# Three orders of work in a masked linear layer with a gated FFN: a gate product behind three sums, the mask counted earlier, and first sums and weight sums moved

## The chip, the cores and the metric

The kernel runs on one core of a Trainium2 chip. The metric is the device time of one execution in microseconds (us); lower is better. Engines are named as the profile names them: PE is TensorE's matmul (PEld its weight load), DVE is VectorE, ACT is ScalarE, POOL is GpSimd and SP is SyncE, which issues almost all DMAs.

## The reference

All data is float32; 2048 rows of 512 features, an FFN with 1792 inner features.

```python
xn = _layernorm(x)
block_mask = mask.reshape(16, 32, 16, 32).astype(float32).sum(axis=(1, 3)) > 0
w_masked = weight * repeat(repeat(block_mask, 32, 0), 32, 1)
s = einsum('bsk,nk->bsn', xn, w_masked)

var = mean(square(xn), -1)
nx = xn * rsqrt(var + 1e-5) * ln_w
h = silu(nx @ gate_w.T) * (nx @ up_w.T)
g = silu(h @ down_w.T)
out = x + s * g
```

## The kernel before

**Tiling.** Every product is cut with two nested levels of a seven-product scheme: a 2x2 block product takes seven block products instead of eight, at the price of sums of blocks before and after. The outer level has seven products, numbered 1, 2, 6, 5, 7, 3, 4; each of them is again seven matmuls of a 128x128 weight block with a 128x512 block of data (m = 1 to 7). One outer product is an "instance" of seven matmuls (`instance`, L392 is its matmul). Gate and up projection and the masked linear layer are laid out alike: seven groups g = 0 to 6 hold the gate and up rows, group 7 is the masked linear layer. First the instances 1 and 2 of all groups run, then the instances 6, 5, 7, 3, 4 group by group. After that comes the down projection (`down_instance`, L640).

**Sums after the products.** An instance adds its matmuls into PSUM banks x, y and z. Between two matmuls of one bank a snapshot of the bank is taken to SBUF (`snap`), after its last one a total (`total`); both are one VectorE instruction of the helper `add` (L98), or a ScalarE copy where nothing is added. The next matmul into a bank whose snapshot is being taken waits for that snapshot. In a group, the quarter (1, 1) of the hidden block needs instance 5 plus instance 7: `summed` (L490) adds those two SBUF tiles, for quarters i = 0 and 1 on VectorE, for i = 2 and 3 on POOL.

**The gate.** When a gate tile and its up tile are there, ScalarE writes silu of the gate into a PSUM bank (`silu`, L458) and VectorE multiplies it with the up tile (`h_out`, L463) and stores the result to DRAM. The key (R, Hh, n) names quarter and column half.

**Order.** The order is written out by hand: `at(pos, fn, ...)` records a function with a position, all records are sorted by position at the end and issued in that order, with a stable order among equals; a manual schedule keeps it. One matmul is one unit of position, `T(us)` turns a time into a position. So a number in an `at` call decides only where an instruction stands in the queue of its engine. The engines run their queues in order and wait for each other by semaphores. DMAs go through SP's queue in the same way.

**Weights.** `load_a` fetches a gate and up tile for instances 1 and 2, `scale_a` (L311 on POOL, L313 on ScalarE) multiplies it with `ln_w`, `inner_a` forms four sums of weight blocks on POOL. A one-element memset on POOL (L739) holds back the loads of the group after the first, since they write the same tile. `load_block` and `outer_a` do the same for the other five instances; `inner_a(g, 2, ...)` then makes four POOL sums over five tiles at once (128x640).

**First data.** The first 1024 rows are normalised in place and transposed on TensorE; `inner_b` (from L779) forms sums of blocks of the transposed data, here partly with an operand in PSUM.

**Mask.** `load_mask` (L344) fetches four 128x512 tiles of the integer mask, `mask_rows` (L349) sums them over 32 columns on VectorE, `mask_blocks` sums over 32 rows by a matmul and compares with zero.

Of the kernel before, what the change touches and what calls it, by code (L numbers as in the profile page):

```python
# [31 lines left out]
def tile_masked_linear_gated_ffn(  # L32
# [36 lines left out]
    def at(pos, fn, *args):  # L69
        events.append((pos, len(events), fn, args))  # L70
# [18 lines left out]
    def slots(i, n):  # L89
        return mem[:, i : i + n, :]  # L90
# [3 lines left out]
    def bank(tag, name):  # L94
        return ps.tile([P, W], F32, tag=tag, name=name, bufs=PSB[tag])

    def add(eng, o, a, b, op=ALU.add):
        eng.tensor_tensor(o, a, b, op)  # L98

    dve, pool, act = nc.vector, nc.gpsimd, nc.scalar  # L100
# [193 lines left out]
    def w_slots(g):  # L294

        return (F["s"], F["s"] + 5) if g % 2 else (F["q"], F["a1"] + 4)
# [59 lines left out]
    def mask_a(v, R, K):  # L356
        v = v.rearrange("p (b j) -> p b j", j=BLK)
        k = keep[:, 2 * R + K, :].unsqueeze(2).to_broadcast([P, 16, BLK])
        nc.gpsimd.tensor_tensor(v, v, k, ALU.mult)

    def inner_a(g, part, k0=0, n=2):

        if part == 1:
            i, si, qs = F["a1"] + 2 * (g % 3), F["s"] + 2 * (g % 2), (1, 2)
        else:
            i, si, qs = *w_slots(g), BLOCKS
        a, s = slots(i + k0, n), slots(si + k0, n)
        a11, a21, a12, a22 = (a[:, :, k * P : (k + 1) * P] for k in range(4))
        s1, s2, s3, s4 = (s[:, :, k * P : (k + 1) * P] for k in range(4))
        for k in range(n):  # L370
            aop[g, qs[k0 + k]] = {1: a11[:, k], 2: a12[:, k], 3: s4[:, k], 4: a22[:, k],
                                  5: s1[:, k], 6: s2[:, k], 7: s3[:, k]}
        return [lambda: add(pool, s1, a21, a22), lambda: add(pool, s2, s1, a11, ALU.subtract),
                lambda: add(pool, s4, a12, s2, ALU.subtract), lambda: add(pool, s3, a11, a21, ALU.subtract)]
# [72 lines left out]
    def group(g, where):  # L447
        def tiles(i):
            return lambda k: mem[:, i + k, :]

        acc, v5, c1 = tiles(F["acc"] + 4 * (g % 2)), tiles(F["v5"] + 4 * (g % 2)), tiles(F["c1"] if g % 2 else F["vc"])
        vc = tiles(F["tmp"] + 2 if g % 2 else F["vc"])
        h11 = tiles(F["a1"])
        gate = {}

        def silu(key, t):
            gate[key] = bank("V", f"gate_{g}_{key[2]}")
            nc.scalar.activation(gate[key], t(), AF.Silu)  # L458

        hs, hpos = {}, {}  # L460

        def h_out(key, a, b, n):
            nc.vector.tensor_mul(a(), gate[key], b())  # L463
            hs[key] = a()
            q = {(0, 0): 1, (1, 0): 2, (1, 1): 3}.get(key[:2])
            if q:
                nc.sync.dma_start(h_dram[HD[q], g, n], a())

        def done(R, Hh, tiles):

            ready = {}

            def after(i, pos):
                r, n = divmod(i, 2)
                if g == G:
                    at(pos + 1, lambda: nc.sync.dma_start(s_dram[2 * R + r, 2 * Hh + n], tiles(i)))
                    return
                ready[i] = pos
                if n in ready and n + 2 in ready:
                    key = (R, Hh, n)  # L480
                    p = max(ready[n] + 1.2, ready[n + 2] - 0.5, SILU)
                    at(p, silu, key, lambda: tiles(n))
                    hpos[key] = max(p, ready[n + 2]) + 1.3
                    at(hpos[key], h_out, key, lambda: tiles(n), lambda: tiles(n + 2), n)
            return after

        def summed(dst, src, into, then=None, engines=(pool,) * 4):

            def after(i, pos):
                at(pos + 1.2, lambda: add(engines[i], into(i), dst(i), src(i)))  # L490
                if then:
                    then(i, pos + 3.2)
            return after

        nothing = lambda i, pos: None
        setup = {
            1: (None, acc, nothing),
            2: (acc, c1, done(0, 0, c1)),
            6: (acc, acc, nothing),
            5: (None, v5, summed(v5, acc, vc)),  # L500
            7: (acc, acc, summed(v5, acc, v5, done(1, 1, v5), (dve, dve, pool, pool) if g < G else (pool,) * 4)),
            3: (vc, vc, done(0, 1, vc)),
            4: (acc, acc, done(1, 0, acc)),
        }
        for q in setup:
            instance(where[g, q], g, q, *setup[q])

        def h_sum(q, n, tile_of, a, b):

            o = hs[q, n] = tile_of()  # L510
            add(pool, o, hs[a + (n,)], hs[b + (n,)], ALU.subtract)
            nc.sync.dma_start(h_dram[HD[q], g, n], o)

        sums, rest = slots(F["acc"] + 4 * (g % 2), 4), 7 * where[g, BLOCKS[0]]
        at(7 * where[g, 1] + 15, lambda: nc.sync.dma_start(acc_dram[g], sums))
        at(rest - (14 if g else 6), lambda: nc.sync.dma_start(sums, acc_dram[g]))
        if g < G:
            def again():
                nc.sync.dma_start(slots(F["a1"], 2), h_dram[HD[1], g].rearrange("n p w -> p n w"))
                hs.update({(0, 0, n): h11(n) for n in range(2)})  # L520
            at(rest + 24, again)
            pos = 0
            for n in (1, 0):
                for q, t, i, a, b in ((5, vc, n + 2, (0, 1), (0, 0)), (7, v5, n + 2, (1, 1), (0, 1)),
                                      (6, vc, n, (1, 1), (5,))):
                    pos = max(pos, hpos[0, 1, n], hpos[1, 1, n]) + 1.45
                    at(pos, h_sum, q, n, lambda t=t, i=i: t(i), a, b)
            for n in (1, 0):
                pos = max(pos, hpos[1, 0, n]) + 1.45
                at(pos, h_sum, 4, n, lambda n=n: acc(n + 2), (1, 0), (6,))  # L530
# [195 lines left out]
    T = lambda us: (us - 14.0) / 0.86  # L726
# [19 lines left out]
    def plan(pos, step, todo):  # L746
        for i, fn in enumerate(todo):
            at(pos + step * i, fn)
# [21 lines left out]
            at(T((8.9, 9.3, 9.8, 11.0)[c] + 0.05 * i), transpose, 0, c, (0, 1, 3, 2)[i], "XYYX"[c])  # L770
            at(T((14.35, 14.8, 15.25, 16.2)[c] + 0.05 * i), transpose, 1, c, (2, 3, 0, 1)[i], "XVVV"[c])
    at(T(6.0), scale_a, 0, 0, pool)
    at(T(10.0), scale_a, 0, 1, pool)
    for c in range(KC):
        at(T((9.75, 10.3, 10.85, 12.05)[c]), evacuate, 0, c, act)
        at((5.6, T(15.6), 6.0, 3.14)[c], evacuate, 1, c, act)
    for pos, q, m, eng in ((1.1, 1, 5, dve), (1.87, 1, 6, dve), (2.56, 1, 7, dve), (3.95, 2, 5, dve), (2.7, 1, 4, pool),
                           (4.6, 2, 6, dve), (7.2, 2, 7, dve), (5.0, 2, 4, pool)):
        at(pos, inner_b, q, m, eng)  # L779
    for q in (1, 2):  # L780
        for k in (0, 1):
# [39 lines left out]
    for g in range(G + 1):  # L821
        p, rest = 7 * where[g, 1], 7 * where[g, BLOCKS[0]]
        for K in range(2):
            if g > 2:
                at(p - 22, load_a, g, K)
            if g == G:
                at(p - (10.4, 7.3)[K], lambda K=K: mask_a(aq[G, 0, K], 0, K))
            elif g > 1:
                at(p - (10.4, 7.3)[K], scale_a, g, K)
        if g:  # L830
            plan(p - 7, 1, inner_a(g, 1))
        else:
            plan(T(9.9), 0, inner_a(0, 1, 0, 1))
            plan(T(11.9), 0, inner_a(0, 1, 1, 1))
        at(rest - 29, load_block, g)

        def block_sums(g=g):
            for k, fn in enumerate(outer_a(g)):
                todo[g, k] = fn
        at(rest - 20, block_sums)  # L840
        if g == G:
            for k, (R, K) in ((1, (1, 0)), (4, (1, 1)), (0, (0, 0)), (3, (0, 1))):
                at(rest - 20.5, lambda k=k, R=R, K=K: mask_a(wblk[G][k], R, K))
        for k, off in enumerate((-19.9, -19.3, -18.1, -17, -15.95, -15.94, -15.93, -15.3, -13.95)):
            at(rest + off, lambda g=g, k=k: todo[g, k]())
        plan(rest - 13, 2.5, inner_a(g, 2, 0, 5))
# [1 line left out]
        for off, fn in zip((8, 24.6, 26.05, 26.06, 26.07, 27.5, 30), outer_d(f)):  # L848
            at(7 * where[f, BLOCKS[0]] + off, fn)
    for i, (R, K) in enumerate(QUADS):  # L850
        at(50, load_mask, R, K)
        at(62 + 3.5 * i, mask_rows, R, K)
    at(79.5, mask_blocks)
    at(120, rms_store)
    for t in range(NTT):
# [10 lines left out]
    def D(o):  # L866
        return lambda k: free[25 * o + k] if 25 * o + k < 25 * len(DOWN) else free[25 * o + k - 1] + 1
# [6 lines left out]
    for o, q in enumerate(DOWN):  # L874
# [24 lines left out]
        for k in range(4):  # L899
            pos = END + (-6, -4.8, 2, 4)[k] if o == 0 else D(o - 1)(10) + 2.5 * k  # L900
# [84 lines left out]
```

## Time and profile before

| | |
|---|---|
| median of 3 runs | 510.52 us (510.2 to 510.72) |
| the profiled execution | 510.38 us, span of its instructions 508.6 us, granted clock 0.999 |
| matmuls of a 128x512 block (L392, L640) | 1126 instructions, two for each product, 0.43 us from start to start |
| VectorE, one 128x512 sum | 0.68 us, 0.60 from start to start |
| POOL, one 128x512 sum of two tiles | 1.27 us |
| POOL, one 128x640 sum of two tiles | 1.54 us |
| mask sums (L349) | 4 of 0.67 us, from 67.2 to 76.7 us |

A row of the timeline gives start, duration, engine, line and operation, `out<-in` by tile names, and `xN` where equal instructions follow each other without another kind between; in brackets the idle time before it and what ended it. Nearly all SBUF tiles lie in one large tile and have the name `mem`; `x`, `y`, `z`, `gate`, `a`, `held` and `pt` are PSUM banks. So `mem<-mem` reads SBUF alone, and `mem<-x,mem` reads a bank and an SBUF tile. Matmul durations overlap; the distance between starts is what counts. The page's line on POOL's and VectorE's busy shares says little about TensorE; its own stalls are seen in the starts of its matmuls.

### The profile page before, as it was taken

The page shows a single profiled execution, that of the slowest core. Times are in us where ns is not written, and L with a number is a line of the kernel's source. Part 1 is how long each engine was busy: PE and PEld are TensorE (multiplying, and loading weights), DVE is VectorE, ACT ScalarE, POOL GpSimd, SP SyncE. Part 2 cuts the span into 40 slices and gives each one's busy share as a digit, 9 for nine tenths or more (in the row PEclk, how much of TensorE's full clock was granted, in tenths as well). Part 3 has the DMA queues.
Part 4 walks back from the last instruction along what each step waited for, and adds up shares of the span by engine and source line. Part 5 has one row for each costly group of instructions (what it writes and reads, how often), then busy time and mean ns, then how long its engine had stood idle before and what let it go on. Part 6 is the DMA issues. An engine that isn't in the chain of part 4 may idle for free. (4 is left out here: it accounts for less than half of the span.)

```text
span 508.6 us, 4930 instructions
## 1 busy us (share of the span) xinstructions
PE 502.6 (99%) x1237; PEld 227.2 (45%) x1237; DVE 376.4 (74%) x583; ACT 188.4 (37%) x361; POOL 358.6 (71%) x300
## 2 busy tenths in 40 slices
PE   8999999999999999999999999999999999999996
PEld 7444434444444444444444444444444444444444
DVE  6978798776978969697796969969747644377636
ACT  5656776634535363352635334330100101001111
POOL 4628997473786959879596889976672764649960
PEclk9999999999999999999999999999999999999999
DMA  6758866269178495866939566599996798467362
GB/s 206 249 189 337 315 227 253 89 256 321 48 242 310 179 309 198 284 250 225 348 145 312 198 236 231 202 337 378 356 343 244 230 394 307 134 247 254 120 226 84
DMA packets 62221, 124.75 MB, mean 245 GB/s; under 512 B 5968, under 2 KB 13552, under 8 KB 60144
## 3 DMA queue, kind: packets, MB, share of 16 engines
q1 hardware_dynamic: 62048, 124.43, 68.6%
q8 instruction: 10, 0.16, 0.1%
q14 instruction: 19, 0.16, 0.1%
q10 hardware_dynamic: 144, 0.00, 0.0%
HBM read 78.25 MB, written 46.15 MB: 245 GB/s over the span
## 5 line engine op out<-in xcount | busy, mean ns | idle before, releaser
L98 POOL TENSOR_TENSOR mem<-mem 128x512 f32<-128x512 f32 (+4 forms) x261 | 322.3, 1258 | 115.1 <-ACT mem L420 32.3
L392 PE MATMUL x<-mem 128*128 128x512 f32 x448 | 213.8, 595 | 0.7 <-DVE mem L98 0.4
L392 PEld LDWEIGHTS x<-mem 128*128 128x128 f32 x448 | 83.8, 190 | 110.3 <-issue 85.8
L98 DVE TENSOR_TENSOR mem<-x,mem 128x512 f32<-128x512 f32 x137 | 92.5, 683 | 42.6 <-PE x L392 39.1
L392 PE MATMUL y<-mem 128*128 128x512 f32 x224 | 114.7, 593 | 0.1
L640 PE MATMUL dx<-mem 128*128 128x512 f32 x174 | 78.3, 592 | 0.0
L98 DVE TENSOR_TENSOR mem<-mem 128x1536 f32<-128x1536 f32 (+3 forms) x50 | 66.3, 1332 | 6.9 <-PE dx L640 4.4
L98 DVE TENSOR_TENSOR mem<-y,mem 128x512 f32<-128x512 f32 x96 | 65.6, 684 | 6.8 <-PE y L392 5.3
L392 PEld LDWEIGHTS y<-mem 128*128 128x128 f32 x224 | 42.2, 190 | 53.7 <-issue 48.3
L399 ACT COPY z<-x 128x512 f32<-128x512 f32 x54 | 30.9, 572 | 91.9 <-PE x L392 88.9
L392 PE MATMUL z<-mem 128*128 128x512 f32 x112 | 57.4, 594 | 0.0
L640 PEld LDWEIGHTS dx<-mem 128*128 128x128 f32 x174 | 33.1, 190 | 41.6 <-issue 40.7
L640 PE MATMUL dy<-mem 128*128 128x512 f32 x98 | 44.5, 592 | 0.0
L463 DVE TENSOR_TENSOR mem<-gate,mem 128x512 f32<-128x512 f32 x56 | 38.1, 682 | 5.9 <-POOL mem L98 3.6
L458 ACT ACTIVATE gate<-mem 128x512 f32<-128x512 f32 x56 | 33.1, 601 | 24.8 <-DVE mem L98 20.3
L613 POOL TENSOR_TENSOR mem<-mem 128x512 f32<-128x512 f32 x16 | 25.6, 1609 | 14.0 <-DMA mem<-s_dram 13.8
L623 ACT ACTIVATE silu<-mem 128x512 f32<-128x512 f32 x15 | 9.0, 602 | 64.6 <-DVE mem L98 48.3
L392 PEld LDWEIGHTS z<-mem 128*128 128x128 f32 x112 | 21.0, 190 | 26.3 <-issue 23.3
L98 DVE TENSOR_TENSOR mem<-z,mem 128x512 f32<-128x512 f32 x41 | 28.0, 683 | 2.8 <-PE z L392 2.7
L640 PEld LDWEIGHTS dy<-mem 128*128 128x128 f32 x98 | 18.6, 190 | 23.4 <-issue 23.2
L98 DVE TENSOR_TENSOR mem<-dx,mem 128x512 f32<-128x512 f32 x16 | 11.1, 691 | 20.5 <-PE dx L640 20.4
L640 PE MATMUL dz<-mem 128*128 128x512 f32 x56 | 25.2, 592 | 0.0
(85 smaller groups left out, 290.3 us busy)
## 6 DMA issues: line engine op xcount, KB each, us to landing
h_dram<-mem SPq DMA_DIRECT2D x98, 256.0 KB, 2.1
mem<-h_dram SPq DMA_DIRECT2D x28, 768.0 KB, 6.3
mem<-in_gu SPq DMA_DIRECT2D x42, 256.0 KB, 3.9
acc_dram<-mem SPq DMA_DIRECT2D x8, 1024.0 KB, 4.3
mem<-acc_dram SPq DMA_DIRECT2D x8, 1024.0 KB, 5.8
mem<-in_x_t SPq DMA_DIRECT2D x24, 256.0 KB, 5.9
mem<-in_x SPq DMA_DIRECT2D x16, 256.0 KB, 4.4
s_dram<-mem SPq DMA_DIRECT2D x16, 256.0 KB, 5.1
```

The source lines that it names most:

```text
L98: eng.tensor_tensor(o, a, b, op)
L392: nc.tensor.matmul(st[key], weights(g, q, m), operand(q, m), start=first and not (key == "z" and seeded), stop=True, skip_group_check=True)
L399: nc.scalar.copy(st["z"], st["x"])
L458: nc.scalar.activation(gate[key], t(), AF.Silu)
L463: nc.vector.tensor_mul(a(), gate[key], b())
L613: at_later.append(lambda: nc.gpsimd.tensor_tensor(s_tile, s_tile, rms_bc[t], ALU.mult))
L623: nc.scalar.activation(b[0][:, part], y[:, part] if source is None else source(), AF.Silu)
L640: nc.tensor.matmul(st[key], w(), b(), start=first and key != "z", stop=True, skip_group_check=True)
```

## The change

Four edits, all of positions, so that only the order in the queues changes, except that two calls of `inner_a` become one.

- In groups 0 to 6 the gate product of key (1, 1, 0) is issued at +3.9 instead of +1.3: behind the z sum, the x snapshot of the next instance and another x sum. Its store to DRAM moves with it, behind one other store on SP.
- The sum of quarter i = 1 on VectorE (instance 5 plus instance 7) is issued at +2.1 instead of +1.2: behind the x snapshot that used to follow it.
- One first data sum (instance 2, m = 7) goes behind the x snapshot that used to follow it. On POOL the scaling of the second weight tile goes ahead of the memset, and the first weight sums, four for each of two tiles (128x128), become four for both tiles at once (128x2x128) behind it.
- The mask loads are issued at positions 15 to 18.6 instead of 50, and the mask sums at 46.1 to 52.6 instead of 62 to 72.5.

```diff
-                    hpos[key] = max(p, ready[n + 2]) + 1.3
+                    hpos[key] = max(p, ready[n + 2]) + (3.9 if key == (1, 1, 0) else 1.3)
                     at(hpos[key], h_out, key, lambda: tiles(n), lambda: tiles(n + 2), n)
...
-                at(pos + 1.2, lambda: add(engines[i], into(i), dst(i), src(i)))
+                at(pos + (2.1 if engines[i] is dve and i == 1 else 1.2), lambda: add(engines[i], into(i), dst(i), src(i)))
...
-    at(T(10.0), scale_a, 0, 1, pool)
+    at(T(9.9), scale_a, 0, 1, pool)
...
-                           (4.6, 2, 6, dve), (7.2, 2, 7, dve), (5.0, 2, 4, pool)):
+                           (4.6, 2, 6, dve), (9.05, 2, 7, dve), (5.0, 2, 4, pool)):
...
-            plan(T(9.9), 0, inner_a(0, 1, 0, 1))
-            plan(T(11.9), 0, inner_a(0, 1, 1, 1))
+            plan(T(11.9), 0, inner_a(0, 1))
...
-        at(50, load_mask, R, K)
-        at(62 + 3.5 * i, mask_rows, R, K)
+        at(15 + 1.2 * i, load_mask, R, K)
+        at((46.1, 48.1, 50.2, 52.6)[i], mask_rows, R, K)
```

## The prediction

> **What bounds the kernel now.** I read the page first, then TensorE's rows in order of time, then the rows of the engine that each late product waited for.
>
> ```profile
> PE 502.6 (99%) x1237; PEld 227.2 (45%) x1237; DVE 376.4 (74%) x583; ACT 188.4 (37%) x361; POOL 358.6 (71%) x300
> ```
>
> TensorE is never idle long enough for the page to show it, so the end moves only with TensorE's stalls. One product (two instructions, 128x512) has a pitch of 0.86 us when nothing holds it: below, 198.15 to 199.86 is 1.71 us for two. The timeline of TensorE in the third group:
>
> ```profile
> 193.85 1.02 PE L392 MATMUL y<-mem 128*128 128x512 f32 x2
> ...
> 198.15 1.88 PE L392 MATMUL x<-mem 128*128 128x512 f32 x4
> 199.86 1.02 PE L392 MATMUL y<-mem 128*128 128x512 f32 x2
> 200.72 2.11 PE L392 MATMUL x<-mem 128*128 128x512 f32 x4
> 202.67 1.02 PE L392 MATMUL y<-mem 128*128 128x512 f32 x2
> ```
>
> Two products from 200.72 take 1.95 us, 0.24 too long. (Each stall has two parts: the wait, here 0.14, and 0.10 lost on the second instruction of the product.) I find this stall once in each of the groups 0 to 5 (141.15, 171.43, 201.71, 231.99, 262.29, 292.57), 1.46 us together; in group 6 two, 0.21 at 314.24 and 0.41 at 323.24; around 70 to 75 us 0.54; and at 23.10 us 0.60. Other stalls after 15 us come to some 0.4: about 3.6 us in all is what a rearrangement could win. VectorE's rows say who holds the one at 201.71:
>
> ```profile
> 198.49 0.68 DVE L463 TENSOR_TENSOR mem<-gate,mem 128x512 f32<-128x512 f32 x1
> 199.77 0.69 DVE L463 TENSOR_TENSOR mem<-gate,mem 128x512 f32<-128x512 f32 x1 [0.60 <-POOL mem L98]
> 200.38 0.68 DVE L98 TENSOR_TENSOR mem<-z,mem 128x512 f32<-128x512 f32 x1
> 200.97 1.28 DVE L98 TENSOR_TENSOR mem<-x,mem 128x512 f32<-128x512 f32 x2
> ```
>
> The gate product of quarter (1,1), n=0, stands at the head of VectorE's queue until POOL has made its other factor (199.73). Behind it stands the first of the two x sums, whose bank TensorE needs at 201.58: it ends at 201.65. VectorE's pitch is 0.60.
>
> **What the Trainium skill says.** "Trainium Architecture — The Big Picture", Inside one NeuronCore: each engine has its own instruction stream and engines meet only through semaphores; the trace agrees, a blocked head holds the rest (0.60 us above). "Perfetto Trace Analysis", Optimization Strategy: find gaps on the contended engine and the semaphore behind each; that is how the list above was made. "SBUF — State Buffer", Who interferes with whom: a VectorE instruction with two SBUF inputs shares a read port with GpSimd, whoever issues first has it for its whole instruction, the other blocks; with one SBUF input there is no contention. The trace of before agrees. A 128x512 sum of two SBUF tiles (first row) and a 128x1536 one (second; 1.75 us where POOL is idle, as at 369.64), and under them the POOL sums that were already running:
>
> ```profile
> 310.73 1.06 DVE L98 TENSOR_TENSOR mem<-mem 128x512 f32<-128x512 f32 x1
> ...
> 360.22 2.55 DVE L98 TENSOR_TENSOR mem<-mem 128x1536 f32<-128x1536 f32 x1
> ...
> 309.96 1.28 POOL L98 TENSOR_TENSOR mem<-mem 128x512 f32<-128x512 f32 x1
> ...
> 358.84 2.31 POOL L98 TENSOR_TENSOR mem<-mem 128x384 f32<-128x384 f32 x1 [0.79 <-PE dy L640]
> ```
>
> POOL ends at 311.24 and 361.15, which is 0.51 and 0.93 after VectorE's start; VectorE lost 0.38 and 0.80. The rest of POOL's instruction less 0.13: this fits all eleven such pairs after 350 us to 0.02, and the one before.
>
> **The change, part by part.** The changed program's order of instructions shows exactly these moves, and no others on TensorE and ScalarE.
>
> *Gate product behind three sums (groups 0 to 6).* After the product that ends at 199.16, the z sum can start at 199.09, the x snapshot 199.69 (ends 200.37, needed at 201.58), the second x sum 200.29, the gate product 200.89 (its factor is there since 199.73), y 201.49. The stall goes: minus 0.24 in each of six groups, minus 0.41 in group 6. The product's readers are late by nothing: POOL takes it at 206.22. Its store passes behind one other store on SP, 2 us later, and is read back only in the last stage. Its PSUM bank is wanted again at 202.88.
>
> *The second VectorE sum behind an x snapshot (same groups; the 2.1 for 1.2).* Before:
>
> ```profile
> 190.79 0.68 DVE L98 TENSOR_TENSOR mem<-a,mem 128x512 f32<-128x512 f32 x1
> 191.39 0.68 DVE L98 TENSOR_TENSOR mem<-mem 128x512 f32<-128x512 f32 x1
> 191.99 0.68 DVE L98 TENSOR_TENSOR mem<-x,mem 128x512 f32<-128x512 f32 x1
> 192.59 0.68 DVE L98 TENSOR_TENSOR mem<-y,mem 128x512 f32<-128x512 f32 x1
> ...
> 191.60 1.87 POOL L98 TENSOR_TENSOR mem<-mem 128x640 f32<-128x640 f32 x1 [0.20 <-PE y L392]
> ...
> 194.66 1.54 POOL L98 TENSOR_TENSOR mem<-mem 128x640 f32<-128x640 f32 x1
> ```
>
> The row at 191.39 adds two SBUF tiles. It starts 0.21 before POOL's weight sum, which is released by the row at 190.79 (end 191.47), so POOL waits (1.87 against 1.54 for the same shape later). Swapped with the row at 191.99, it starts at 191.99, 0.39 after POOL, which then holds the port to 193.14. By the rule above the sum loses 193.14 - 191.99 - 0.13 = 1.02 and ends at 193.69; the y snapshot starts at 193.61 instead of 192.59 and ends at 194.29. The y product at 193.85 waits for it: it starts at 194.34, plus 0.10 on its second half, 0.59 in all. What follows on VectorE is 1.02 late but has more than that until TensorE, itself 0.59 later, asks (the x snapshot of the first part: 201.39 against 202.17). The sum's own readers have slack (ScalarE's gate at 192.16 would come at 193.72; its product is at 196.09).
>  So plus 0.59 for groups 1 to 5; group 0, whose POOL sum starts 0.08 earlier against VectorE, 0.96 held and 0.53. Group 6: the x snapshot comes early, so its stall of 0.21 goes, but the y product due at 315.00 gets its bank at 315.80: 0.86 + 0.10 = 0.96.
>  Bounds on the hold: nothing, if the two do not collide here, and 1.15, the whole overlap; I take 1.02, from the fit.
>
> *First sums (9.05 for 7.2).* The sum at 21.67 goes behind the x snapshot at 22.27. The product that waited to 23.10 starts at 22.50 (its predecessor's pitch). The y snapshot behind is done at 23.55 instead of 23.75, so y starts at 23.61 rather than 24.03, loses 0.10 and the next product starts at 24.57, not 24.89: minus 0.32. Bounds: 0 to minus 0.43.
>
> *First weight sums.* POOL loses four sums of 128x128 (1.94) between its two scalings, does the second scaling as soon as its tile lands (11.35), and then four sums of 128x2x128 (0.73 each, by the same shape at 22.47) instead of four of 128x128. The two products at 12.91 and 13.88 come 0.25 and 0.36 earlier, and gain nothing: the transposes behind them wait for VectorE's normalising (14.97), which does not move. The sums end at 16.4, wanted at 16.63 (first one, 14.1) to 19.75. But the memset that releases the next 12 loads moves from 11.85 to about 13.25: loads 1.4 us later. First takers: ScalarE's scaling at 16.54 (landed 14.67, now 16.07) and VectorE's statistics at 24.26 (22.38, now 23.8). Both still covered; cost 0, up to 0.5 if the landings slip.
>
> *Mask.* Four reductions of 0.60 leave 67 to 77 us and go to 53 to 60. There VectorE has gaps of 1.08 and 0.75 for the first three; the fourth pushes the sums behind it by 0.6, and the x snapshot that ended at 61.32 with 0.70 to spare now ends at 61.94, just in time (cost 0 to 0.15). In the old place the stalls at 72.68 (0.23) and 74.9 (0.08) go. The one at 69.87 (0.23) stays: it is ScalarE's unbroken queue from 64.63, which starts 0.12 later because VectorE frees a bank later. Net minus 0.19; bounds minus 0.54 and plus 0.15. The four loads (1 MB) move from 57.7 to about 20 to 26 on SP, ahead of two weight loads and the x loads: DMA share is 0 at 24 and 30 us and 0.05 from 35 to 38, so I price them at nothing; without that cover POOL's scaling at 40.68 would be late.
>
> **Sum.** Groups: 0.53 + 5 x 0.59 + 0.96 = 4.44 new, 1.46 + 0.62 = 2.08 gone: plus 2.36. With minus 0.32 and minus 0.19: plus 1.85 us. Against the profiled execution (510.38 us, span 508.6) 512.2; the median of the runs is 510.52, 0.14 above, so I say 512.3.
>
> **Rivals.**
> A. No collision: POOL and VectorE interleave, or VectorE's sum is held under 0.5 us, so the y product has its bank in time. Then 2.08 + 0.32 + 0.19 = 2.6 goes: 507.8, faster. For it: the trace has one 128x512 case only, and that was held 0.38. Against: POOL was nearly done there, and the rule fits both shapes.
> B. A partial hold: above 0.54 us the y product begins to wait; at 0.7 it costs 0.16 + 0.10 in each group, all in all about the 2.08 gained, so with head and mask 510.1 to 510.5, no change. It needs a port that POOL lets go some 0.3 before its sum ends, which no pair in the trace shows.
> C. The loads: memset and masks together late enough that POOL's scaling (40.68) slips over 1 us and VectorE's sums at 62 wait, about 0.5 to 1 us more: 513. Against: the idle DMA time above.
>
> **Numbers.** My case 0.74, A 0.12, B 0.07, C 0.07. About 0.2% (1.0 us) is what can be told from no change. My case alone runs from 511.3 to 513.1 (hold 0.9 to 1.15, head and mask at their bounds), and its lower edge counts as no change for 0.02. C stretches the top to 513.2. Range 511.3 to 513.2. Slower: 0.72 + 0.07 = 0.79; same: 0.02 + 0.07 = 0.09; faster 0.12.
>
> **What would show it.** Right: the SBUF-only sum in each group has 1.6 to 1.7 us, POOL's first 128x640 sum 1.54, TensorE shows about 0.6 at the y product (193.85 in before's time) and nothing at 201.71; at 23 us nothing; at 72 to 75 nothing. Wrong: if that sum keeps 0.68, A is so and the time is near 507.8; if stalls show at 62 us, the mask's place costs more than I gave it.

## The result, and the profile after

Median 512.94 us (512.54 to 513.28, 5 runs) against 510.72 us (510.2 to 510.79, 5 runs): ratio 1.0046, 95% interval 1.0031 to 1.006, so slower by 0.5%, clear of the noise. The profiled execution took 513.28 us, span 511.5. It was the slowest of its five, and the profiled one of before (510.38) lay below its median, so the spans differ by 2.9 us where the medians differ by 2.2.

In the third group, VectorE and POOL of the changed kernel (timeline: start, duration, engine, line and operation):

```profile
191.94 0.68 DVE L98 TENSOR_TENSOR mem<-a,mem 128x512 f32<-128x512 f32 x1
192.54 0.68 DVE L98 TENSOR_TENSOR mem<-x,mem 128x512 f32<-128x512 f32 x1
193.13 1.70 DVE L98 TENSOR_TENSOR mem<-mem 128x512 f32<-128x512 f32 x1
194.76 0.68 DVE L98 TENSOR_TENSOR mem<-y,mem 128x512 f32<-128x512 f32 x1
...
192.75 1.54 POOL L98 TENSOR_TENSOR mem<-mem 128x640 f32<-128x640 f32 x1 [0.20 <-PE y L392]
```

The sum of two SBUF tiles, 0.68 us before, starts 0.38 after POOL's weight sum and takes 1.70: it lost 1.02, or was held, as such a loss beside a POOL instruction is called below. POOL, first now, has its 1.54 again (1.87 before). TensorE of the same kernel:

```profile
193.29 1.88 PE L392 MATMUL x<-mem 128*128 128x512 f32 x4
195.49 1.12 PE L392 MATMUL y<-mem 128*128 128x512 f32 x2 [0.33 <-DVE mem L98]
196.45 1.88 PE L392 MATMUL x<-mem 128*128 128x512 f32 x4
198.17 1.02 PE L392 MATMUL y<-mem 128*128 128x512 f32 x2
...
202.46 1.88 PE L392 MATMUL x<-mem 128*128 128x512 f32 x4
204.18 1.02 PE L392 MATMUL y<-mem 128*128 128x512 f32 x2
```

From 193.29 to 195.49 two products take 2.20 instead of 1.72, and the y product itself 0.96 instead of 0.86: 0.59 lost. The two x products from 202.46 take 1.72, so the old stall of 0.24 is gone. All groups read alike: 0.55 in group 0, 0.59 to 0.60 in groups 1 to 5, 0.97 in group 6, together 4.49 new for 2.08 gone.

At 70 us one stall is left, 0.17 at the z product and 0.10 after it (70.67 for 70.50), where before had 0.54 between 67 and 77; with a new 0.08 at 63.64 that is minus 0.18:

```profile
69.64 1.02 PE L392 MATMUL y<-mem 128*128 128x512 f32 x2
70.67 1.12 PE L392 MATMUL z<-mem 128*128 128x512 f32 x2
71.64 1.88 PE L392 MATMUL x<-mem 128*128 128x512 f32 x4
73.35 1.02 PE L392 MATMUL y<-mem 128*128 128x512 f32 x2
```

The head differs from what was foreseen. First before, then after: VectorE normalising the second 512 rows (L153) and POOL's weight sums beside it.

```profile
14.01 1.97 DVE L153 TENSOR_SCALAR mem<-mem,scl,nb 128x256 f32<-128x256 f32 x4
...
13.84 1.99 POOL L98 TENSOR_TENSOR mem<-mem 128x128 f32<-128x128 f32 x4
```

```profile
13.92 3.05 DVE L153 TENSOR_SCALAR mem<-mem,scl,nb 128x256 f32<-128x256 f32 x4
16.89 1.48 DVE L98 TENSOR_TENSOR mem<-pt,mem 128x512 f32<-128x512 f32 x2
...
13.75 3.08 POOL L98 TENSOR_TENSOR mem<-mem 128x256 f32<-128x256 f32 x4
```

The same four instructions of VectorE take 3.05 instead of 1.97, beside four POOL sums of twice the width. VectorE's first sums start at 16.89 for 15.90, and the y product that needs them follows. TensorE of before, and then of the changed kernel, where the bracket gives the idle time and its releaser:

```profile
16.63 1.13 PE L392 MATMUL y<-mem 128*128 128x512 f32 x2
...
23.10 1.10 PE L392 MATMUL x<-mem 128*128 128x512 f32 x2 [0.43 <-DVE mem L98]
24.03 1.02 PE L392 MATMUL y<-mem 128*128 128x512 f32 x2
24.89 1.45 PE L392 MATMUL x<-mem 128*128 128x512 f32 x3
```

```profile
15.48 1.14 PE L162 MATMUL pt<-ident,mem 128*128 128x128 f32 x8 [0.46 <-DVE mem L153]
17.02 0.55 PE L162 MATMUL pt<-ident,mem 128*128 128x128 f32 x3 [0.40 <-DVE mem L153]
17.71 1.10 PE L392 MATMUL y<-mem 128*128 128x512 f32 x2
...
22.62 1.97 PE L392 MATMUL x<-mem 128*128 128x512 f32 x4
24.60 1.12 PE L392 MATMUL y<-mem 128*128 128x512 f32 x2
25.56 1.88 PE L392 MATMUL x<-mem 128*128 128x512 f32 x4
```

The y product that started at 16.63 starts at 17.71, a loss of 1.08; the transposes (L162) ahead of it waited twice for the normalising. The stall at 23.10 is gone (22.62 to 24.60 holds two products), the y product behind waits a little, as foreseen; the next product starts at 25.56 for 24.89, plus 0.67. Plus 0.67, minus 0.18 and plus 2.41 make the 2.9 of the spans.

### The profile page after: what moved, and what is told of

The parts are those of the page before. It is cut to its first block, busy times and chain, and to the rows that moved or that the text cites. A ratio compares the mean times of both kernels' runs of the same rounds, so it can differ in the third digit from the quotient of the medians.

```text
span 511.5 us, 4933 instructions
## 1 busy us (share of the span) xinstructions
PE 502.2 (98%) x1237; PEld 226.9 (44%) x1237; DVE 383.6 (75%) x583; ACT 188.5 (37%) x361; POOL 359.0 (70%) x296
## 5 line engine op out<-in xcount | busy, mean ns | idle before, releaser
L98 POOL TENSOR_TENSOR mem<-mem 128x512 f32<-128x512 f32 (+3 forms) x257 | 322.7, 1278 | 116.0 <-ACT mem L420 33.8
L98 DVE TENSOR_TENSOR mem<-mem 128x1536 f32<-128x1536 f32 (+3 forms) x50 | 73.2, 1468 | 6.9 <-PE dx L640 4.4
L640 PEld LDWEIGHTS dy<-mem 128*128 128x128 f32 x98 | 18.6, 190 | 23.4 <-issue 23.0
```

What stands on the lines that cost most here:

```text
L640: nc.tensor.matmul(st[key], w(), b(), start=first and key != "z", stop=True, skip_group_check=True)
```

## The experiments

Each run is compared with runs of the kernel before on the same chip, whose medians were 510.29 to 510.41. All edits are made to the kernel before unless it says "changed kernel".

**The sum alone.**

```diff
-                at(pos + 1.2, lambda: add(engines[i], into(i), dst(i), src(i)))
+                at(pos + (2.1 if engines[i] is dve and i == 1 else 1.2), lambda: add(engines[i], into(i), dst(i), src(i)))
```

> The kernel before with only the second VectorE sum behind the x snapshot; the gate product keeps its place. Theory (POOL's 128x640 sum locks it out; 1.0 us later on VectorE, POOL's factor of the gate product is there in time anyway): sum 1.6 to 1.7 us, y product 0.59 late in each group, stall at the gate product gone by itself, groups plus 2.4 as in the changed kernel: 512.9. Rival 1 (costs and gains add up, the product's move is worth 1.9 in either order): plus 4.4, 514.9. Rival 2 (the product's move makes the loss): no change, 510.5.

Measured: 513.21 us, ratio 1.0055 (1.0042 to 1.0069). VectorE of this run:

```profile
192.13 0.68 DVE L98 TENSOR_TENSOR mem<-x,mem 128x512 f32<-128x512 f32 x1
192.72 1.71 DVE L98 TENSOR_TENSOR mem<-mem 128x512 f32<-128x512 f32 x1
...
200.26 1.28 DVE L463 TENSOR_TENSOR mem<-gate,mem 128x512 f32<-128x512 f32 x2
201.45 0.68 DVE L98 TENSOR_TENSOR mem<-z,mem 128x512 f32<-128x512 f32 x1
```

The hold is the one of the changed kernel. The two gate products stand one behind the other with no idle time between: VectorE arrives 1.0 us later, POOL's factor is there, and the stall that the product's move was to remove is gone without it. Costs and gains do not add up here: rival 1 is out by 1.7 us, rival 2 by 2.7.

**The gate product alone.**

```diff
-                    hpos[key] = max(p, ready[n + 2]) + 1.3
+                    hpos[key] = max(p, ready[n + 2]) + (3.9 if key == (1, 1, 0) else 1.3)
```

> The kernel before with only the gate product of (1,1,0) behind three sums. Theory: the stall of 0.24 in groups 0 to 5 and of 0.41 in group 6 goes, nothing comes in its place: minus 1.87, 508.7. Rival (the stall only moves to the next VectorE reader, or POOL waits for the product): 510 to 510.5.

Measured: 508.60 us, ratio 0.9964 (0.9952 to 0.9977), minus 1.8. On VectorE the z sum and the two x sums now go ahead, and the gate product finds its factor:

```profile
198.67 0.68 DVE L98 TENSOR_TENSOR mem<-z,mem 128x512 f32<-128x512 f32 x1
199.27 1.28 DVE L98 TENSOR_TENSOR mem<-x,mem 128x512 f32<-128x512 f32 x2
200.46 0.69 DVE L463 TENSOR_TENSOR mem<-gate,mem 128x512 f32<-128x512 f32 x1
```

No stall is left in groups 0 to 5; the 0.2 at the start of group 6 stays. So the move is good by itself; beside the moved sum, which alone removes the same stalls (the run above), it has nothing left to win there.

**POOL's weight sum cut in two.** Both group edits, and in groups 0 to 6:

```diff
-        plan(rest - 13, 2.5, inner_a(g, 2, 0, 5))
+        if g < G:
+            plan(rest - 13, 0, [inner_a(g, 2, 0, 2)[0], inner_a(g, 2, 2, 3)[0]])
+            plan(rest - 10.5, 2.5, inner_a(g, 2, 0, 5)[1:])
+        else:
+            plan(rest - 13, 2.5, inner_a(g, 2, 0, 5))
```

> The kernel before with both group edits (gate product behind three sums, second VectorE sum behind the x snapshot), and POOL's first 128x640 weight sum of each group cut in two instructions, 128x256 and 128x384. Theory (the hold is the rest of the POOL instruction that was running less 0.13): POOL's first part lasts 0.73, of which 0.34 is left when VectorE's sum starts, so it is held 0.2 and takes 0.9 instead of 1.7; the y product has its bank in time; only the gains of 2.08 are left: 508.3. Rival (VectorE waits until POOL has nothing more to do, or for the second part too): sum 1.6 us or more, groups plus 2.4, 512.8.

Measured: 509.66 us, ratio 0.9985 (0.9979 to 0.9992). Faster than before, but 1.4 above the expectation. The timeline of VectorE and POOL in this run, third group first, then group 6:

```profile
191.53 0.68 DVE L98 TENSOR_TENSOR mem<-mem 128x512 f32<-128x512 f32 x1
...
190.91 0.73 POOL L98 TENSOR_TENSOR mem<-mem 128x256 f32<-128x256 f32 x1
...
312.07 1.71 DVE L98 TENSOR_TENSOR mem<-mem 128x512 f32<-128x512 f32 x1
...
311.69 1.54 POOL L98 TENSOR_TENSOR mem<-mem 128x640 f32<-128x640 f32 x1 [0.21 <-DVE mem L98]
```

In groups 0 to 5 the sum has its 0.68. The overlap is smaller than I assumed: POOL's first part doesn't need the last of the weight tiles, starts 0.62 ahead of VectorE and has only 0.11 left. POOL's second part starts at 191.59, 0.06 behind VectorE's sum, and it is POOL that waits: this 128x384 sum takes 1.48, where one of that shape took 0.99 at 419.07 in the kernel before. In group 6 the sum meets the weight sum of group 7, which was not cut: again 1.71, and 0.97 lost at the y product. That is most of the miss: minus 1.46 for groups 0 to 5, plus 0.97 minus 0.62 in group 6, minus 1.1 in all, as the spans have it (507.5 against 508.6). The other 0.4 lies outside the span: the runs of this kernel take 2.2 us more than their spans, those of before 1.8, and no run here says why. The same execution so shows the sum free where POOL's short instruction is nearly over, and held where the long one has just begun.

**The first weight sums alone, and only their scaling moved.** The first has both edits; the second keeps eight sums of 128x128:

```diff
-    at(T(10.0), scale_a, 0, 1, pool)
+    at(T(9.9), scale_a, 0, 1, pool)
...
-            plan(T(9.9), 0, inner_a(0, 1, 0, 1))
-            plan(T(11.9), 0, inner_a(0, 1, 1, 1))
+            plan(T(11.9), 0, inner_a(0, 1))
```

```diff
-    at(T(10.0), scale_a, 0, 1, pool)
+    at(T(9.9), scale_a, 0, 1, pool)
...
-            plan(T(9.9), 0, inner_a(0, 1, 0, 1))
+            plan(T(11.9), 0, inner_a(0, 1, 0, 1))
```

> The kernel before with only the edit of the first weight sums (scaling of the second tile ahead of the memset, four sums of 128x2x128 for eight of 128x128). Theory (the longer POOL sums hold VectorE's normalising): the four L153 rows take 0.7 to 0.9 us each again, the y product after them is about 1.0 us late, and as the stall at 23.10 stays in this kernel (it is released by VectorE, which is 1.0 late too) all of it stays: 511.3 to 511.6, plus 1.0. Rival (the head lost its time to the other head edit or to the mask loads): 510.5, L153 rows as before.

> The kernel before with the scaling of the second tile ahead of the memset and both tiles' sums behind it, but the sums left as eight of 128x128. The loads come 1.4 us later as in the changed kernel. Theory (it is the length of one POOL sum that counts, because VectorE gets in only between two of them): L153 rows 0.45 to 0.6 us, head within 0.3 us of before, 510.5 to 510.8. Rival (POOL's later work or the later loads cost it): plus 1.0 us, 511.5.

Measured: 511.21 us, ratio 1.0015 (1.0009 to 1.0022), and 510.73 us, ratio 1.0005 (0.9997 to 1.0013). The weight sums alone cost 0.8, a little less than the 1.0 expected; with narrow sums at the same late place and the same late loads 0.36 remains, which its interval can't tell from nothing. The statistics of L153 (shortest, median and longest instruction in ns) in the first:

```profile
L153 DVE TENSOR_SCALAR mem<-mem,scl,nb x4: 400/610/901, 14.5 to 16.4; 128x256 f32<-128x256 f32 x4
```

and in the second:

```profile
L153 DVE TENSOR_SCALAR mem<-mem,scl,nb x4: 543/578/630, 14.2 to 15.7; 128x256 f32<-128x256 f32 x4
```

In the first the second weight tile landed early, so POOL's wide sums lay earlier (12.91 to 15.98) and covered only the first two of the four; the last two took 0.40. The wide sums also held two small instructions ahead (128x4), 0.74 and 0.32 for about 0.17 each.

**No POOL sum beside the normalising.**

```diff
-            plan(T(11.9), 0, inner_a(0, 1, 1, 1))
+            plan(2.75, 0, inner_a(0, 1, 1, 1))
```

> The kernel before with the second tile's first weight sums (four of 128x128) moved on POOL behind the 128x512 sum at 17.46, so that POOL has no sum while VectorE normalises the second 512 rows. Theory (a POOL sum locks VectorE's normalising out): the four L153 rows take 0.25 to 0.35 us each instead of 0.44 to 0.61, VectorE's first sums start 0.8 us earlier, the y product at 16.63 comes up to 0.6 earlier: 509.8 to 510.2. Rival (the 0.44 to 0.61 are the instruction's own time): rows unchanged, 510.4 or, if the weight sums are then late, more.

Measured: 510.50 us, ratio 1.0000 (0.9992 to 1.0008), no gain where 0.2 to 0.6 was expected. The instruction's own time:

```profile
L153 DVE TENSOR_SCALAR mem<-mem,scl,nb x4: 409/410/415, 14.0 to 15.0; 128x256 f32<-128x256 f32 x4
```

So 0.41 alone (I had said 0.25 to 0.35), 0.44 to 0.63 beside narrow sums, 0.71 to 0.90 beside wide ones: VectorE is held here by POOL's sums, and by each for as long as that one runs. The time did not follow: VectorE was done at 15.40 instead of 15.98, yet the y product came at 16.59. VectorE's first sum then waited 0.45 for TensorE's transposes and the second 0.36 for ScalarE's copy, and ScalarE's half of the normalising ended at 16.10 as before. TensorE itself was late in this execution: its first transposes began at 9.94 (9.11 before), and from 11.26 to the y product it shows no idle time. So a faster VectorE found TensorE busy and ScalarE no earlier. This is read from one execution; that the other twelve went the same way is not shown.

**The rest of the change.** Mask and first sums as in the change, nothing else.

> The kernel before with only the mask's new places and the first sum of instance 2, m = 7 behind the x snapshot; the first weight sums as before. Theory: the stall at 23.10 becomes two small ones (minus 0.32), the stalls at 72 to 75 go (minus 0.18): 509.9, minus 0.5. Rival (the early mask loads or the new order of the first sums cost the time at the head): 510.7 to 511.0.

Measured: 509.91 us, ratio 0.9991 (0.9983 to 0.9999), minus 0.5. TensorE of this run has the shape foreseen at 23 us (x products at pitch, y 0.24 late, next at 24.52):

```profile
21.60 1.96 PE L392 MATMUL x<-mem 128*128 128x512 f32 x4
23.56 1.13 PE L392 MATMUL y<-mem 128*128 128x512 f32 x2
24.52 1.88 PE L392 MATMUL x<-mem 128*128 128x512 f32 x4
```

**The changed kernel with one losing edit undone.**

> The changed kernel with the first weight sums as before (scaling at its old place, eight sums of 128x128). Theory: the y product at 17.71 is back at about 16.6 and the gain of the first-sum order is kept: groups plus 2.4, mask minus 0.18, head minus 0.3, so 512.3, which is 0.6 to 1.0 below the changed kernel. Rival (the early mask loads are part of the loss at the head): 512.9, as the changed kernel.

> The changed kernel with the second VectorE sum at its old place. Theory: the gate product's move then brings its 1.87, the stall of 0.2 at 314 us in group 6 is back, head plus 0.5 to 0.7, mask minus 0.18: 508.9 to 509.3, some 4 below the changed kernel. Rival (part of the loss in the groups comes from the product's move or its store): 510 or more.

Measured, without the weight sums' edit: 512.58 us (511.94 to 512.66), ratio 1.0041 (1.0027 to 1.0054). That is 0.36 below the changed kernel, less than the 0.6 to 1.0 expected, and the intervals overlap; against the kernel before, each as measured beside it, both are slower by the same 2.2 to 2.3 us. So the times don't settle this run. The profile fits the theory: it has the y product at 16.52 and the product after the stall's place at 24.71, 0.85 ahead of the changed kernel. Without the sum's edit: 508.73 us, ratio 0.9968 (0.9956 to 0.9981), 4.2 below the changed kernel and slightly better than expected.

**Versions without the losing edits.** First: gate product, mask and first sums. Second: that, with the weight sums moved apart as above. Third: the first, with the moved sum and POOL's weight sum cut in all eight groups:

```diff
-        plan(rest - 13, 2.5, inner_a(g, 2, 0, 5))
+        plan(rest - 13, 0, [inner_a(g, 2, 0, 2)[0], inner_a(g, 2, 2, 3)[0]])
+        plan(rest - 10.5, 2.5, inner_a(g, 2, 0, 5)[1:])
```

> The changed kernel with both losing edits undone: the gate product behind three sums, the mask's new places, the first sum behind the x snapshot. Theory: minus 1.87, 0.18 and 0.32: 508.0, as with the weight sums moved apart as well.

> The parts that should gain, together: gate product behind three sums, mask's new places, first sum behind the x snapshot, and the second tile's first weight sums behind the 128x512 sum on POOL; the second VectorE sum and the scaling as in the kernel before. Theory: minus 1.87 in the groups, minus 0.18 at the mask, minus 0.3 to 0.9 at the head: 507.4 to 508.0. Rival (head and mask gains are lost again before the groups): 508.5, as with the gate product alone.

> The same, but with the second VectorE sum behind the x snapshot and POOL's first 128x640 sum of all eight groups cut in 128x256 and 128x384. In the run with the cut in seven groups the sum met no POOL instruction for long in groups 0 to 5 (0.68 us) and the loss of 0.97 at the y product of group 6 stayed. Theory: it goes too, and the stall of 0.2 at 314 us with it: minus 2.08, 0.18 and 0.32: 507.8. Rival (the parts' waits shift and another sum is held): 508.0 to 509, stalls at other products.

| version | median us | ratio to before, 95% |
|---|---|---|
| first | 508.07 | 0.9959 (0.9947 to 0.9972) |
| second | 508.09 | 0.9951 (0.9938 to 0.9965) |
| third | 508.10 | 0.9954 (0.9941 to 0.9966) |

All three beat both kernels by more than 2 us and are one and the same within their intervals; the extra edits of the second and third pay nothing that can be seen in the time. The third, expected at 507.8, has no stall left between 130 and 350 us, but came out at 508.10. In it the sum in group 6 takes 0.67 and its y product is on time, which completes the result on the cut:

```profile
311.48 0.67 DVE L98 TENSOR_TENSOR mem<-mem 128x512 f32<-128x512 f32 x1
...
311.26 1.88 PE L392 MATMUL x<-mem 128*128 128x512 f32 x4
312.98 1.02 PE L392 MATMUL y<-mem 128*128 128x512 f32 x2
```

## Why the prediction was right, and where not

The time, 512.94, lies in the range and 0.6 above the forecast. The sum was plus 1.85; the profile has plus 2.9, the medians plus 2.2. The large term, the held sum, was foreseen with its cause and its size. One small term was not. The total still fell inside, with 0.26 to spare, because that term is small beside the groups; the profiled execution, 513.28, lies just above the range.

- **Second VectorE sum: right.** The hold was to be 1.02 and is 1.02; 4.44 was to be lost at the y products, 4.49 was. The sum alone shows it, and the cut of POOL's instruction takes it away. Rivals A and B (no hold, a partial one) are refuted by 1.70 in the groups.
- **Gate product: right in size, and only half right in cause.** The 2.08 is gone, and the product's move alone brings 1.8. But in the changed kernel the moved sum would have removed these stalls anyway; I counted the gain once, so the total holds, but put it down to the product.
- **First sums and mask: right.** Both together, run alone, brought 0.5 (priced 0.51); the mask's part is 0.18 in the profile (priced 0.19). Rival C, late loads, doesn't show: near 62 us, where it was to be seen, there is 0.08 at 63.64, inside the bound given to the mask. POOL's instruction at 40.68, on which that rival rested, starts at 41.32, no later than all that stands behind the head (0.67).
- **First weight sums: the step that failed.** The sentence was that the transposes "wait for VectorE's normalising (14.97), which does not move". It moved: four instructions from 1.97 to 3.05 us, and with them the y product by 1.08. Priced at 0 with 0.5 as the upper bound, the edit cost 0.8 by itself (511.21) and 0.7 by the medians of a pair with and without it (508.73 against 508.07). I had applied the shared port to sums of two SBUF tiles alone, and wrote that "with one SBUF input there is no contention". The section that I cited (the Trainium skill, "SBUF — State Buffer", Who interferes with whom) says so only of instructions outside the two-port modes. It also lists `tensor_scalar`, the operation of L153, among the operations that can take both ports in a two-port mode and then contend. The trace agrees that it contends: 0.41 without POOL's sums, up to 0.90 beside them. Whether L153 runs in such a mode, no run here shows, and its speed speaks against it: alone it takes 0.41, with 0.33 from start to start, just as a 128x256 sum of a bank and a tile does (194.38 in the kernel before). So what lets it contend stays open; that it does is measured. The row of before held the hint, 439 to 612 ns for equal instructions. The gain ahead of it was smaller than said, too: POOL's second scaling began at 11.84, not 11.35, and the two products at 12.91 and 13.88 came 0.10 earlier, not 0.25 and 0.36.
- **Total.** The head was to gain 0.32 and lost 0.67 in the profiled execution; that 1.0 is nearly the whole difference between 1.85 and 2.9. The medians differ by less because that execution was 0.34 above its median and the one of before 0.34 below the median measured beside it. Part of such a spread may come from the head: how many of the four instructions meet a wide sum goes with when the second weight tile lands. POOL's scaling of it began at 11.84 in the profile of the changed kernel (all four held), at 11.19 without the sum's edit (three), at 11.00 with the weight sums alone (two). With one profile of each kernel, how often each case comes is not shown.

## What to carry to other kernels

Before an instruction of VectorE or POOL is moved, list for both its old and its new place which instruction of the other engine is running and which of the two starts first. Equal instructions with unequal durations in the trace can mark such a place, as the four of L153 did here. Making POOL's sums wider is not free where VectorE works beside them: the four of L153 ended 0.15 after the sum beside them, however long it was. And gains of two moves in one queue must be tested apart and together: the delay from one can do the work of the other.

## What the runs showed of the hardware

A VectorE instruction held by one of POOL's sums ends a fixed time after that sum. The two-tile sum of 128x512 ended 0.55 after it in all seven groups (in the third, POOL ended at 194.29, the sum at 194.83). The 128x256 `tensor_scalar` ended 0.15 after it, whether POOL's sum was 128x128 or 128x256. The last pair of before and of the changed kernel:

```profile
15.43 0.54 DVE L153 TENSOR_SCALAR mem<-mem,scl,nb 128x256 f32<-128x256 f32 x1
...
15.32 0.51 POOL L98 TENSOR_TENSOR mem<-mem 128x128 f32<-128x128 f32 x1
```

```profile
16.16 0.81 DVE L153 TENSOR_SCALAR mem<-mem,scl,nb 128x256 f32<-128x256 f32 x1
...
16.04 0.78 POOL L98 TENSOR_TENSOR mem<-mem 128x256 f32<-128x256 f32 x1
```

Ends: 15.97 against 15.83, and 16.97 against 16.82. Even instructions over 128x4 were held by a wide sum, 0.74 us instead of 0.17. A sum with one operand in a PSUM bank was not: the y and z sums at 194.76 and 195.36 took 0.68 and 0.67 while POOL's next sum ran (from 194.25, for 1.72).

When the two engines start almost together, the order of their rows does not tell who waits. The second of the four normalising instructions starts at 14.54 in the changed kernel and POOL's sum at 14.55, and VectorE was held (0.88). With 0.06 between them, VectorE's two-tile sum at 191.53 ahead of POOL's at 191.59, in the run with the cut weight sum, it was POOL that waited.

The hold is not always a whole instruction of POOL. Beside POOL's scaling (L311, 0.93 for 128x256) two instructions that began in its first half were let go near its middle. In the changed kernel the scaling ran from 12.74 to 13.66, and the 128x4 instruction beside it from 12.95 to 13.23, 0.28 instead of 0.17. In the kernel before the two started together at 12.82, and the 128x4 instruction took 0.50.
